# A preparation row of a fused attention, expert and slot kernel begins five turns later and is cut into seven pieces

## The chip, the cores and the metric

The kernel runs on one core of a Trainium2 chip. The metric is device time in microseconds (us) of one execution of the whole kernel. The profile is one execution taken by the hardware profiler; all positions in it are microseconds from the start of its span. The engines are named as the profile names them: PE (TensorE matmuls), PEld (TensorE weight loads), DVE (VectorE), ACT (ScalarE), POOL (GpSimd), SP (SyncE, which here only issues transfers).

## The reference, cut to what matters

`x` has 2048 tokens of 256 numbers, `ctx` has 1601 rows of 256. Four residual steps follow one another:

```python
x = x + cross_attention(layernorm(x), ctx)            # 16 heads, first stage
x = x + top1_of_8_experts(layernorm(x))               # second stage
x = x + windowed_attention(ctx, layernorm(x))         # third stage
x = x + slot_mixture(layernorm(x))                    # fourth stage
```

The third stage looks only at rows of `ctx` within 16 of a centre `p_t`, weighted by a Gaussian:

```python
mask = (idx < max(p_t - 16, 0)) | (idx > min(p_t + 16, src_len))
score = where(mask, -1e9, q @ W_a @ ctx.T)
align = softmax(score) * exp(-(idx - p_t)**2 / 128)
out = tanh(concat([align @ ctx, q]) @ W_c.T)
```

`p_t` and `src_len` are one number each, so everything that depends on them and on `ctx` alone (the window's rows, the mask, the Gaussian, the product of the rows with `W_a` and with `W_c`) is the same for all tokens. The kernel computes these tables once.

## The kernel before, in words

**Attention.** The first part of `body` runs to L909. Its last steps, after the last `weigh` (L907), are taken from a list `later` (L908): the last head group is transposed and divided (L798, L799), turned (L811 to L815), multiplied with `WoT` in two halves (L824), and each half is added to `x_sb` (L829). Both halves use the one PSUM buffer of `small()`, so the second half's matmuls wait until L829 has read the first half.

**The loads of the later stages.** SP issues 14 loads (L930 to L945). POOL issues the small ones (L947 to L965), among them `slen_i` (L947) and `pt` (L948, issued by the helper at L83).

**Experts, with rows beside them.** From L1400 the kernel walks five blocks of tokens: three of 4 x 128 tokens and two of 2 x 128 (`BLOCKS`, L967). `experts(lb)` (L1031) handles one 128-token tile at a time, in four pairs of experts. For one pair PE does two fp32 matmuls of 128x512 (four records in the profile, L1041) into one of four PSUM buffers, and DVE adds both experts to `x_sb` with two instructions (L1048). After each pair the generator yields. Behind every second tile an expert bias is added (L1059, L1061). A PSUM buffer comes free when L1048 or L1061 has read it.

Each yield of `experts` is one **turn**. In a turn, `aside(3)` (L1391) takes up to three rows (generators) from the front of the list `beside`, lets each do its next piece, and puts them at the end again. A row that ends does not count among the three. Nothing else sets the order: every engine executes its instructions in the order in which these pieces emit them. Only the end of attention and the beginning of this part are interleaved with one another when the program is built; the trace shows on each engine which came first. The rows are:

- `front(lb + 1)` (L1020): prepares the next block for the experts. Two pieces of layer-norm statistics (L990; DVE, then one POOL instruction L102 for the reciprocal root), two pieces that apply them (L995, which is L107 on DVE), two pieces that transpose on PE (L1002), two for the router (`route`, L147).
- `window()` (L1069): the tables of the third stage. This is the function that the change edits.
- `slots()` (L1246): tables of the fourth stage, in 7 pieces, added after block 0.
- `after(windowed(lb), weights(lb))`: the third stage and the fourth stage's weights of a block whose experts are done, added after each block. `windowed` reads the tables of `window` at L1194, in its seventh piece.

The rows that are left when the experts end are worked off one piece at a time (L1413), and the final slot computation and the output follow (L1416 to L1530).

**`window()` before.** Piece 1 (L1071 to L1094): `slen`, the window's limits `lo`, `hi` and `base` from `slen_i` and `pt` (seven DVE instructions, L1072 to L1083); the row numbers `at_i` (POOL iota L1086, DVE L1088 to L1090); and the gather of 64 rows of `ctx` with an indirect DMA issued by POOL (L1092). Piece 2 (L1112 to L1121): mask and Gaussian over the window's 64 rows. Piece 3 (L1124 to L1138): the same over all 1601 rows. Then empty turns. Then `eT` (L1142 to L1149: transposes of the gathered rows), `outside` (L1151 to L1158: 26 matmul records that sum all rows of `ctx`), `oT` and `m` (L1161 to L1178), and `evw` (L1180 to L1185). The pieces 1 to 3 run in turns 1 to 3, `eT` in turn 10, `evw` in turn 13.

Of the kernel before, what the change touches and what calls it, by code (L numbers as in the profile page):

```python
# [62 lines left out]
def body(ctx: ExitStack, tc: tile.TileContext, a: dict, out: bass.AP):  # L63
# [1004 lines left out]

    def window():  # L1069

        slen = late.tile([P, 1], F32, name="slen")  # L1071
        nc.vector.tensor_copy(slen, slen_i)  # L1072
        lo = late.tile([P, 1], F32, name="lo")
# [7 lines left out]
        base_i = late.tile([P, 1], I32, name="base_i")  # L1081
        nc.vector.tensor_copy(base_i, base)
        nc.vector.tensor_copy(base, base_i)  # L1083

        at_i = late.tile([NW, 1], I32, name="at_i")
        nc.gpsimd.iota(at_i, pattern=[[0, 1]], base=0, channel_multiplier=1)  # L1086
# [10 lines left out]
        def in_window(pos, n, name):  # L1097

            t = late.tile([P, n], F32, name=name)
            nc.vector.tensor_scalar(t, pos, lo, None, ALU.is_ge)  # L1100
            nc.vector.scalar_tensor_tensor(t, pos, hi, t, ALU.is_le, ALU.mult)
            return t

        def gauss(pos, n, name):
            t = late.tile([P, n], F32, name=name)
            nc.vector.tensor_scalar_sub(t, pos, pt)
            nc.vector.tensor_tensor(t, t, t, ALU.mult)
            nc.scalar.activation(t, t, AF.Exp, scale=-1.0 / 128.0)
            return t
# [4 lines left out]
        posr = late.tile([P, NW], F32, name="posr")  # L1114
        nc.vector.tensor_copy(posr, posr_i)
        nc.vector.tensor_scalar_add(posr, posr, base)
        inr = in_window(posr, NW, "inr")
        gr = gauss(posr, NW, "gr")
        neg = late.tile([P, 1, NK], F32, name="negw")
        nc.vector.tensor_scalar(neg[:, 0, :NW], inr, -1.0, 3e38, ALU.add, ALU.mult)  # L1120
# [9 lines left out]
        nc.gpsimd.iota(row_i, pattern=[[P, NS]], base=0, channel_multiplier=1)  # L1130
        row = late.tile([P, NS], F32, name="row")
        nc.vector.tensor_copy(row, row_i)
        ins = in_window(row, NS, "ins")
        gs = gauss(row, NS, "gs")
        nc.vector.tensor_scalar(ins, ins, -1.0, 1.0, ALU.mult, ALU.add)
# [1 line left out]
        one = late.tile([1, 1], F32, name="one")  # L1137
        nc.gpsimd.memset(one, 1.0)  # L1138

        for _ in range(7):  # L1140
            yield
        eT = late.tile([P, 2, NW], F32, name="eT")  # L1142
        gET = late.tile([P, 2, NK], F32, name="gET")
# [243 lines left out]

    NB = len(BLOCKS)
    beside = [window()]

    def aside(n):  # L1391
# [218 lines left out]
```

## Time and profile before

| what | value |
|---|---|
| time, median of 3 runs | 1083.15 us (1083.15 to 1085.77) |
| the profiled execution's own time | 1085.9 us |
| its span | 1084.1 us |
| PE busy in the span | 961.7 us (89%) |
| DVE busy in the span | 749.3 us (69%) |
| attention's last `acc` matmuls (L849) on PE | from 798.05 to 800.50 us |
| block 0's first pair of experts starts on PE | 800.40 us |
| block 0's last bias (L1059) starts on PE | 857.43 us |
| first addition of block 1 (L1048) | 860.44 us |
| first addition of block 2 (L1048) | 911.92 us |

A line of a timeline gives the start, the duration, the engine, the line of the kernel, the operation with its output and inputs, how many were merged, and in square brackets how long the engine had been idle and what ended that. In the chain of waits each line is a piece of the chain that ended last: start, length, engine and what it did. Tables by stretch give for each engine the busy time and the number of instructions, and then the clock that TensorE was granted (1.00 is full), the share of the DMA engines that was busy, and the GB/s.

### The profile page before, as it was taken

To read this page: it belongs to the slowest core of one execution; us is meant where nothing else is said; L and a number is where in the kernel's file an instruction comes from. 1 tells how busy PE (TensorE), PEld (TensorE's weight loads), DVE (VectorE), ACT (ScalarE), POOL (GpSimd) and SP (SyncE) were. 2 spreads that over 40 slices of the span, in tenths; PEclk is the share of its full clock that TensorE was granted. 3 is DMA by queue.
4 is the path that set the end of the run, shared out by engine and by line. 5 is a ranking of instruction groups with operands and counts; after the bars stand their busy time and mean duration, and the time that the engine had idled before them with its cause. 6 is when DMAs were issued, how large, how long until landed. Compare 5 with 4: busy or idle time off the path is not lost.

```text
span 1084.1 us, 14756 instructions
## 1 busy us (share of the span) xinstructions
PE 961.7 (89%) x5742; PEld 448.1 (41%) x5742; DVE 749.3 (69%) x1415; ACT 516.9 (48%) x614; POOL 71.9 (7%) x96
## 2 busy tenths in 40 slices
PE   6787888989989899898889989899997999999986
PEld 2234333444443343343334434344343455545543
DVE  6456867878777787878787876977016566675754
ACT  2423546666646565656566665665840011221331
POOL 4000200000010000001000000000020003021210
PEclk8777979999999999999999999998998999999999
DMA  4763721310102100001210110100033000000002
GB/s 157 162 150 93 145 71 44 107 27 3 28 2 71 60 13 28 16 13 28 88 29 2 28 28 2 28 2 1 2 108 116 1 1 0 1 1 1 1 0 78
DMA packets 32277, 46.96 MB, mean 43 GB/s; under 512 B 6412, under 2 KB 21269, under 8 KB 31951
## 3 DMA queue, kind: packets, MB, share of 16 engines
q1 hardware_dynamic: 30478, 43.65, 15.0%
q10 hardware_dynamic: 1232, 1.61, 0.4%
q8 instruction: 45, 0.74, 0.3%
q0 software_dynamic: 496, 0.76, 0.3%
q14 instruction: 26, 0.21, 0.1%
HBM read 26.77 MB, written 14.04 MB: 38 GB/s over the span
## 4 chain that ended last, share of the span: by engine, by line
PE 67%; DVE 24%; issue 4%; DMA 2%; ACT 1%; POOL 1%; SPq 0%; POOLq 0%; DVEq 0%; ACTq 0%
PE acc L849 18%; PE s_ps L883 14%; DVE mx L262 12%; PE a_ps L257 11%; PE y_ps L1041 7%; PE a_ps L240 2%; DVE xn L107 2%; DVE x_sb L1048 2%; PE a_ps L498 1%; PE a_ps L824 1%; PE o_ps L1227 1%; DVE ln_stats L96 1%; PE a_ps L284 1%; PE x_ps L461 1%; PE a_ps L461 1%
## 5 line engine op out<-in xcount | busy, mean ns | idle before, releaser
L262 DVE TENSOR_REDUCE mx<-a_ps 128x2 f32<-128x804 f32 (+1 forms) x645 | 494.2, 799 | 133.9 <-PE a_ps L257 123.4
L888 ACT ACTIVATE es<-s_ps 128x1024 f32<-128x1024 f32 (+1 forms) x416 | 405.6, 1021 | 231.8 <-PE s_ps L883 225.0
L257 PE MATMUL a_ps<-kb,qb 50*128 50x402 bf16 x992 | 235.3, 353 | 47.7 <-DVE mx L262 32.5
L883 PE MATMUL s_ps<-qt,kt 52*128 52x512 f32 (+1 forms) x832 | 242.4, 530 | 2.1 <-DMA qt<-nT 2.1
L849 PE MATMUL acc<-es,v 128*32 128x512 f32 (+1 forms) x1664 | 233.0, 632 | 0.0
L257 PEld LDWEIGHTS <-qb 50*128 50x128 bf16 x1024 | 81.2, 95 | 294.6 <-issue 276.3
L883 PE MATMUL s_ps<-ql,kt 52*128 52x512 f32 (+1 forms) x832 | 196.9, 403 | 0.0
L883 PEld LDWEIGHTS s_ps<-qt,kt 52*128 52x128 f32 (+1 forms) x832 | 102.9, 196 | 29.2 <-ACT es L888 16.1
L883 PEld LDWEIGHTS s_ps<-ql,kt 52*128 52x128 f32 (+1 forms) x832 | 108.5, 192 | 0.4
L1041 PE MATMUL y_ps<-expert_wT_sb,xT 128*128 128x512 f32 x192 | 89.8, 598 | 0.0
L102 POOL TENSOR_TENSOR ln_rstd<-ln_ve,mhalf 128x2 f32<-128x2 f32 (+2 forms) x28 | 21.1, 754 | 781.3 <-DVE ln_ve L100 780.0
L1048 DVE SCALAR_TENSOR_TENSOR x_sb<-y_ps,r_gate,x_sb 128x256 f32<-128x256 f32 x96 | 46.3, 482 | 32.5 <-PE y_ps L1041 30.7
L849 PEld LDWEIGHTS acc<-es,v 128*32 128x32 f32 (+1 forms) x1664 | 33.4, 109 | 54.5 <-issue 52.9
L1041 PEld LDWEIGHTS y_ps<-expert_wT_sb,xT 128*128 128x128 f32 x192 | 34.1, 191 | 31.9 <-issue 30.8
L1004 ACT COPY xT<-tr_ps 128x512 f32<-128x512 f32 (+1 forms) x28 | 13.4, 493 | 53.3 <-PE tr_ps L1001 53.3
L798 DVE RECIPROCAL rec<-a_ps 128x16 f32<-128x16 f32 x16 | 4.1, 258 | 49.4 <-PE a_ps L240 49.4
L107 DVE TENSOR_SCALAR xn<-x_sb,ln_mv,ln_rstd 128x256 f32<-128x256 f32 x64 | 32.8, 554 | 1.1 <-POOL ln_rstd L102 1.1
L1041 PE MATMUL y_ps<-expert_wT_sb,xnT 128*128 128x512 f32 x64 | 32.2, 631 | 0.0
L1001 PE MATMUL tr_ps<-ident,xn 128*128 128x128 f32 x88 | 17.6, 296 | 10.9 <-DVE xn L107 10.9
L284 PE MATMUL a_ps<-ident,nsp 128*8 128x128 f32 x64 | 10.0, 279 | 19.3 <-DVE nsp L275 18.9
L96 DVE BATCH_NORM_STATS2 ln_stats<-x_sb 128x6 f32<-128x256 f32 x64 | 23.3, 413 | 3.4 <-POOL x_sb L1235 3.4
L1048 DVE SCALAR_TENSOR_TENSOR x_sb<-y_ps,gate,x_sb 128x256 f32<-128x256 f32 x32 | 15.4, 483 | 13.6 <-PE y_ps L1041 13.0
(343 smaller groups left out, 727.9 us busy)
## 6 DMA issues: line engine op xcount, KB each, us to landing
qt<-q_rows SPq DMA_DIRECT2D x32, 192.0 KB
q_rows<-qhi SPq DMA_DIRECT2D x8, 512.0 KB
qb<-q_rows SPq DMA_DIRECT2D x30, 96.0 KB
kt<-expert_wT_sb SPq DMA_DIRECT2D x24, 100.5 KB
q_rows<-qp SPq DMA_DIRECT2D x8, 256.0 KB
q_rows<-qlo SPq DMA_DIRECT2D x8, 256.0 KB
ql<-q_rows SPq DMA_DIRECT2D x32, 64.0 KB
expert_wT_sb<-in_expert_wT SPq DMA_DIRECT2D x1, 2048.0 KB
```

The lines of the kernel that those rows point to most:

```text
L96: nc.vector.bn_stats(stats[:rows, i, :], src[:, i, :])
L102: nc.gpsimd.tensor_tensor(rstd[:rows, :n], ve[:rows, :n], mhalf[:rows, :n], ALU.pow)
L107: nc.vector.tensor_scalar(dst[:, i, :], src[:, i, :], mv[:rows, i, 0:1], rstd[:rows, i : i + 1], ALU.subtract, ALU.mult,)
L240: nc.tensor.transpose(ps[:, t * P : (t + 1) * P], src[:, t, c * P : c * P + n], ident)
L257: nc.tensor.matmul(ps[:, k, :CH], qb[u % 2][rows, pl, t * P : (t + 1) * P], kb[g][rows, pl, c * CH : (c + 1) * CH], start=True, stop=True,)
L262: nc.vector.tensor_reduce(flat[:, n : self.n], ps[:, : self.n - n, :CH], AX.X, ALU.max)
L461: nc.tensor.matmul(ps[:n, :D], ctxT[:, c, i * P : i * P + n], wv[:, c, :], start=c == 0, stop=c == 1,)
L849: nc.tensor.matmul(acc[HP * j : HP * (j + 1), :], v[:n, i, h * VW : h * VW + HP], es[j // 2][:n, j % 2, :], start=i == 0, stop=i == NS - 1,)
L883: nc.tensor.matmul(ps[:n, h, :], kt[u % NG][rows, pl, i * P : i * P + n], q[u % nq][rows, pl, :], start=k == 0, stop=k == 1,)
L888: nc.scalar.activation(e[:n], ps[:n], AF.Exp)
L1041: nc.tensor.matmul(ps.rearrange("p e d -> p (e d)"), xT[:, c, tok], ew[:, c, pair * 2 * D : (pair + 1) * 2 * D], start=c == 0, stop=c == 1,)
L1048: nc.vector.scalar_tensor_tensor(xb[:, t, :], ps[:, k, :], gate[:, t, e : e + 1], xb[:, t, :], ALU.mult, ALU.add,)
```

## The change

`window()` first yields five times with nothing done. Its three pieces of tables become seven: the limits alone; the row numbers and the gather; the positions; the mask; the Gaussian; the sums and the positions of all rows; their mask and Gaussian. The run of yields ahead of `eT` is cut from seven to four. No instruction is added, removed or given another size.

```diff
     def window():
 
+
+        for _ in range(5):
+            yield
         slen = late.tile([P, 1], F32, name="slen")
...
         nc.vector.tensor_copy(base, base_i)
+        yield
 
         at_i = late.tile([NW, 1], I32, name="at_i")
...
         nc.vector.tensor_scalar_add(posr, posr, base)
+        yield
         inr = in_window(posr, NW, "inr")
+        yield
         gr = gauss(posr, NW, "gr")
...
         nc.vector.tensor_copy(row, row_i)
+        yield
         ins = in_window(row, NS, "ins")
...
-        for _ in range(7):
+        for _ in range(4):
             yield
         eT = late.tile([P, 2, NW], F32, name="eT")
```

## The prediction

> **What bounds the kernel now.** I read the busy shares first (PE 89%, DVE 69%), then the chain of waits, then the stretch where the edited row stands. PE is the longest engine almost everywhere, so time can only be won where PE stands still. The slices of the page show PE falling to 7 tenths beside the start of the expert stage, near 810 us. The chain of waits from 800 to 832 us:
>
> ```profile
> 800.52 0.59 ACT osb L787
> 801.13 0.78 POOL slen_i L947
> 801.91 6.94 DMA pt_b<-in_pt
> ...
> 809.78 0.61 DVE x_sb L829
> 810.43 2.01 PE a_ps L824 x8
> ...
> 823.33 0.80 PE tr_ps L1001 x2
> 824.13 3.41 PE y_ps L1041 x4
> 827.54 0.83 PE tr_ps L1001 x4
> 828.37 1.72 PE y_ps L1041 x4
> 830.09 1.69 PE r_ps L155 x16
> ```
>
> The chain leaves PE for a tiny transfer (`pt`, 6.94 us) and returns to it for good only at 823.33. Also, four matmuls of a pair take 3.41 us at 824.13 and 1.72 us at 828.37. The timeline of PE names the idle time:
>
> ```profile
> 810.43 1.99 PE L824 MATMUL a_ps<-WoT_sb,aT 128*128 128x256 f32 x8 [1.45 <-DVE x_sb L829]
> 820.02 0.65 PE L1001 MATMUL tr_ps<-ident,xn 128*128 128x128 f32 x2 [3.72 <-DVE xn L107]
> 823.33 0.80 PE L1001 MATMUL tr_ps<-ident,xn 128*128 128x128 f32 x2 [2.66 <-DVE xn L107]
> ```
>
> All three waits are for DVE. The timeline of DVE says why it is late:
>
> ```profile
> 808.02 0.15 DVE L1072 CAST slen<-slen_i 128x1 f32<-128x1 int32 x1 [2.89 <-DMA slen_i<-in_slen]
> 808.88 0.15 DVE L1074 TENSOR_SCALAR lo<-pt_b 128x1 f32<-128x1 f32 x1 [0.70 <-DMA pt_b<-in_pt]
> ...
> 814.01 0.99 DVE L1048 SCALAR_TENSOR_TENSOR x_sb<-y_ps,gate,x_sb 128x256 f32<-128x256 f32 x2
> ```
>
> Piece 1 of `window` stands in DVE's queue ahead of both L829 and of the second pair's additions (814.01, though PE had that pair done near 805). DVE waits for two transfers with everything behind it. Last, the table by stretch (clock is third from the end):
>
> ```profile
> 816.30:820.00 3.70, 0.00 (x0) 0.00 (x0) 2.74 (x11) 0.26 (x1) 0.95 (x6) 1.00 1.01 344
> 820.00:823.30 3.30, 0.65 (x2) 0.28 (x2) 2.92 (x14) 0.68 (x2) 0.00 (x0) 0.71 0.95 285
> 823.30:828.30 5.00, 4.97 (x11) 2.66 (x12) 1.86 (x5) 0.58 (x1) 0.00 (x0) 0.51 0.02 5
> ```
>
> PE's two pauses are followed by 5 us at half clock. From 830.09 to 857.43 (the block's last bias) the chain is PE without a pause, 27.34 us; block 1 (860.4 to 911.9) has only 1.6 us of PE idle.
>
> **The opening of block 0 after the change.** Turns 1 to 5 carry nothing of `window`. I lay out DVE and PE with the trace's durations: pair 1.72 us on PE, its two additions 1.0, statistics of two tiles 1.25 (0.74 + 0.30 + 0.2), applying them 0.73, L829 0.69.
>
> - PE runs as before to the end of the first L824 half, near 808.0. DVE has meanwhile done pair 1 and the second statistics (805.2 to 807.5), so L829 runs at 808.05 instead of 809.70 and the second L824 half starts near 808.9 instead of 810.43: 1.5 us won. Should L829 stand behind one more addition, 1.0 of this is lost.
> - PE goes on: second half to 810.8, pair 3 to 812.5, gate transposes to 813.0, pair 4 to 814.75.
> - The first transposes need the first applied tiles, and these need POOL's reciprocal root. This is the next thing that is late:
>
> ```profile
> 812.63 0.13 POOL L1240 MEMSET xn<- 128x16 f32 x1 [0.34 <-PE a_ps L824]
> 812.70 0.73 POOL L102 TENSOR_TENSOR ln_rstd<-ln_ve,mhalf 128x2 f32<-128x2 f32 x1
> ```
>
> This is the first of two roots; before, the second waited for DVE until 816.16. The first can hardly start earlier, because POOL issues loads until 812.30 and that doesn't change. With the second directly behind it, the roots end at about 813.1 and 813.85. DVE: apply 813.2 to 813.9, pair 3's additions to 814.9, second apply to 815.6. PE: first two transposes at 814.75, the others at 815.65, done at 816.0 with 0.55 us of idle time.
> - Then pair 5, transposes, pair 6: 1.72 + 0.6 + 1.72, so `r_ps` starts near 820.0 against 830.09. PE's own work from 800.4 to there checks it: 7 pairs 12.0, L240 1.8, L824 3.9, gate 0.5, transposes 1.2, in all 19.4, so 819.8 without any idle time.
>
> The winnings are 1.5 (L824) + 3.72 + 2.66 - 0.55 = 5.8 (pauses) + 2.4 (the clock), 9.7 us.
>
> For the clock, the row says PE worked 4.97 us at 0.51, so 2.4 us is lost. The Trainium skill ("TensorE: Matmul & The Clock Gate", Part 1: The HAM clock gate) says half clock comes after an idle window of some 3.4 us and goes after some 3.4 us of sustained work; by that 1.7 us would be lost, and the sum would be 9.0. I take the row.
>
> A rule speaks against this. The skill ("SBUF — State Buffer", two separate sides) says DVE and POOL share a port pair as an exclusive lock, and POOL cannot write descriptors while certain DVE instructions run. DVE is now to work from 805 to 812 while POOL issues loads, where it used to wait. By the rule, each of POOL's five issues from 808.28 to 811.75 could wait for one DVE instruction, up to 0.5 us each: root 2.5 us later, transposes at 816.5 or so, gain 7.5. But the rows show POOL's issues at 0.53 to 0.56 us from 802.46 to 805.11, where DVE ran additions and statistics, and 0.52 to 0.55 where it stood. I take zero, and keep 2.5 for the range.
>
> **Where the removed work lands.** The seven pieces come in turns 6 to 12. Their DVE time by start-to-start distances: limits 1.0, row numbers 0.5, window tables 1.56, all-row tables 1.75, in all 4.8 us. Cover: PE in turns 6 to 12 has 7 pairs 12.0, transposes 0.6, router 1.7, bias 1.1 = 15.4. DVE there has additions 6.7, router 1.95, bias 0.7 and the 4.8, 14.1. It fits, with four PSUM buffers of slack; adding turn by turn, DVE is at most some 3 us behind PE (turn 12). Cost zero; without cover 4.8. The transfers `slen` and `pt` landed by 808.9, the limits now run near 819: no wait.
>
> The gather moves from POOL at 814.37 to near 823, behind the loads and roots instead of between the two roots (one reason why the second was late). Its issue takes 1.01 us and it lands in 6.7; `eT` reads it nine turns later, at least 15 us. SP's 14 loads keep their place and are all issued by 818.7; nothing of `window` stands in SP's queue. Cost zero. If the gather took over 15 us, PE would wait for the rest.
>
> `eT` moves from turn 10 to turn 16, and `outside`, `oT`/`m`, `evw` (PE 5.71 + 0.53 + 1.03 + 0.86 = 8.13 us) from turns 11 to 13 to turns 17 to 20, block 1. PE is the bound in both blocks, so this only moves. There is one new wait: DVE's copy of `outside` stood idle 4.70 us for PE in block 0, which had room. In block 1, `slots` and statistics of the third stage queue behind it. DVE in turns 17 to 22: six pairs' additions 5.7 (0.95 each), four statistics 5.0, four applies 2.9, `slots` 2.8 (L1250 to L1278), `window` 1.3, bias 0.7, wait 4.7 = 23.1. PE: six pairs 10.3, `window` 8.1, `slots` 5.2, bias, gate and transposes 3.4 = 27.0. It fits: zero, if not, up to 4.7.
>
> In turns 17 to 20 four rows share three visits per turn, so `front`, `slots` and the third stage each fall one turn back. Counting visits, block 0's row ends in turn 42 instead of 41 and from turn 43 the order is the old one. The tail is the same instruction for instruction: zero. Block 1's 1.6 us of PE idle may partly fill: up to 1.6 more.
>
> **Rivals.** (1) *DVE becomes the bound in turns 6 to 12*: all 4.8 us reach the path; gain 4.9, 1078.3. Against it: 14.1 under 15.4. (2) *The interleaving puts an L829 behind the first apply, which waits for POOL's root*: L829 at 813.9, second L824 half at 814.6, PE idle 5.7 us and perhaps half clock again; gain 2 to 5, about 1079.5. Against it: in the trace both L829 come before instructions that waited for POOL. (3) *Slower*: DVE waits for `outside` in block 1 with the densest DVE stretch behind it. Price 4.7, with 4.8 uncovered in block 0 and one pair's time (1.72) for rows that fall back: 11.2 against 9.7, +1.5, 1084.7. It decides once PE's waits for DVE in turns 6 to 24 pass 9.7 us. Against it: 23.1 under 27.0. (4) *Nothing changes*, because the first root is the real bound: then PE would still reach `r_ps` near 830. Against it: that root ended at 813.43 and PE was free from 816.3, yet the transposes came at 820.02.
>
> **How the numbers follow.** The profiled execution took 1085.9 (span 1084.1, 1.8 around it): less 9.7 is 1076.2. It lies 2.75 above the median, to which I apply the same difference: 1083.15 - 9.7 = 1073.4. Chances: full gain (7.5 to 12) 0.72; rival 1 or 2, gain 3.3 to 7.5, 0.19; about no change 0.04; slower 0.05. A difference under 0.3% (3.2 us) can't be told from none. The range goes from 1070.5 (idle of block 1 filled too, 1.6, and a little DVE smoothing) to 1079.0 (rival 1 and most of 2).
>
> **What would show it.** Right: no DVE wait for `slen` or `pt`; L829 near 808; `tr_ps` starting near 815 with idle below 1 us; no stretch at 0.5 clock from 815 to 830; `r_ps` near 820; `out_ps` behind block 1's first pair; the first addition of block 2 near 902. Wrong: PE waiting for L1048 in turns 7 to 13 (rival 1), L829 at 813 or later (rival 2), PE idle after `out_ps` (rival 3), `r_ps` near 830 (rival 4).

## The result, and the profile after

Median time after 1077.57 us (1077.25 to 1077.90, four runs) against 1083.79 before (four runs): ratio 0.9938, interval 0.9911 to 0.9965. Forecast was 1073.4 with a range of 1070.5 to 1079.0. The profiled execution after took 1077.58 us, its span is 1075.8.

The chain of waits after the change, from the end of attention (start, length, what):

```profile
802.92 1.06 PE y_ps L1041 x2
...
808.76 1.81 PE a_ps L824 x8
...
811.43 1.92 PE a_ps L824 x8
...
817.22 0.44 PE tr_ps L1001 x4
817.66 1.72 PE y_ps L1041 x4
819.38 0.44 PE tr_ps L1001 x4
819.81 1.72 PE y_ps L1041 x4
821.53 1.69 PE r_ps L155 x16
```

PE never leaves the chain. From the first pair of experts to the router it takes 18.5 us (802.85 to 821.37 in PE's timeline); before it took 29.5 (800.40 to 829.92). The table by stretch for the same three windows as before (clock third from the end):

```profile
816.30:820.00 3.70, 3.70 (x16) 2.01 (x15) 2.43 (x7) 0.74 (x2) 0.00 (x0) 1.00 1.11 296
820.00:823.30 3.30, 3.30 (x21) 2.50 (x20) 2.21 (x10) 0.43 (x1) 0.00 (x0) 1.00 1.05 366
823.30:828.30 5.00, 5.00 (x14) 2.17 (x14) 3.91 (x19) 0.23 (x1) 1.36 (x5) 1.00 0.49 152
```

No pause and full clock. DVE's timeline shows where the waits went (line numbers after the edit are 3 to 7 higher below L1068; the limits are L1075 on):

```profile
810.61 0.69 DVE L829 TENSOR_TENSOR x_sb<-x_sb,a_ps 128x512 f32<-128x512 f32 x1 [1.06 <-PE a_ps L824]
...
814.92 0.73 DVE L107 TENSOR_SCALAR xn<-x_sb,ln_mv,ln_rstd 128x256 f32<-128x256 f32 x2 [0.85 <-POOL ln_rstd L102]
...
820.33 0.14 DVE L1075 CAST slen<-slen_i 128x1 f32<-128x1 int32 x1
...
849.00 0.41 DVE L1165 COPY outside<-out_ps 1x256 f32<-1x256 f32 x1 [3.62 <-PE out_ps L1161]
```

L829 waits for PE alone, the limits wait for nothing, and the copy of `outside` now waits in block 1. POOL's first root, the next thing expected to be late, comes 11.3 us after the first pair of experts (12.3 before), and the second follows it at once:

```profile
814.06 0.15 POOL L1247 MEMSET xn<- 128x16 f32 x1
814.13 1.55 POOL L102 TENSOR_TENSOR ln_rstd<-ln_ve,mhalf 128x2 f32<-128x2 f32 x2
```

**Two measures of the same change.** The first pair of experts starts at 802.85 after and at 800.40 before, though up to there both are the same program. Counted from that pair, the rest takes 283.70 us before (1084.1 - 800.4) and 272.95 after: 10.75 won. The two profiled times differ by 8.3, because 2.45 went ahead of the edited code. Most experiments below are therefore read from the first pair on, and their medians stand beside it.

### The profile page after: what moved, and what is told of

It is laid out like the page before. It is cut to its first block, busy times and chain, and to the rows that moved or that the text cites. A ratio compares the mean times of both kernels' runs of the same rounds, so it can differ in the third digit from the quotient of the medians.

```text
span 1075.8 us, 14758 instructions
## 1 busy us (share of the span) xinstructions
PE 960.7 (89%) x5742; PEld 448.5 (42%) x5742; DVE 750.1 (70%) x1415; ACT 517.2 (48%) x614; POOL 72.0 (7%) x96
## 3 DMA queue, kind: packets, MB, share of 16 engines
q10 hardware_dynamic: 1232, 1.61, 0.4%
## 4 chain that ended last, share of the span: by engine, by line
PE 70%; DVE 22%; issue 4%; DMA 1%; ACT 1%; SPq 1%; POOL 0%; POOLq 0%; DVEq 0%; ACTq 0%
PE acc L849 18%; PE s_ps L883 14%; DVE mx L262 12%; PE a_ps L257 11%; PE y_ps L1041 8%; PE a_ps L240 2%; PE a_ps L824 2%; PE a_ps L498 1%; DVE xn L107 1%; PE o_ps L1234 1%; DVE x_sb L1048 1%; DVE ln_stats L96 1%; PE a_ps L284 1%; PE x_ps L461 1%; PE a_ps L461 1%
## 5 line engine op out<-in xcount | busy, mean ns | idle before, releaser
L849 PE MATMUL acc<-es,v 128*32 128x512 f32 (+1 forms) x1664 | 232.7, 631 | 0.0
L1048 DVE SCALAR_TENSOR_TENSOR x_sb<-y_ps,r_gate,x_sb 128x256 f32<-128x256 f32 x96 | 46.3, 482 | 37.9 <-PE y_ps L1041 36.0
L849 PEld LDWEIGHTS acc<-es,v 128*32 128x32 f32 (+1 forms) x1664 | 33.4, 109 | 54.3 <-issue 52.8
L107 DVE TENSOR_SCALAR xn<-x_sb,ln_mv,ln_rstd 128x256 f32<-128x256 f32 x64 | 33.2, 562 | 1.9 <-POOL ln_rstd L102 1.9
L1041 PE MATMUL y_ps<-expert_wT_sb,xnT 128*128 128x512 f32 x64 | 29.6, 597 | 0.0
L96 DVE BATCH_NORM_STATS2 ln_stats<-x_sb 128x6 f32<-128x256 f32 x64 | 23.4, 413 | 3.4 <-POOL x_sb L1242 3.4
L262 DVE TENSOR_REDUCE mx<-s_ps 128x2 f32<-128x804 f32 x16 | 15.9, 994 | 12.5 <-PE s_ps L257 12.5
L974 PE MATMUL busy_ps<-xnT 128*128 128x512 bf16 x95 | 24.2, 387 | 0.0
```

The costliest lines, as they stand in the source:

```text
L96: nc.vector.bn_stats(stats[:rows, i, :], src[:, i, :])
L107: nc.vector.tensor_scalar(dst[:, i, :], src[:, i, :], mv[:rows, i, 0:1], rstd[:rows, i : i + 1], ALU.subtract, ALU.mult,)
L262: nc.vector.tensor_reduce(flat[:, n : self.n], ps[:, : self.n - n, :CH], AX.X, ALU.max)
L849: nc.tensor.matmul(acc[HP * j : HP * (j + 1), :], v[:n, i, h * VW : h * VW + HP], es[j // 2][:n, j % 2, :], start=i == 0, stop=i == NS - 1,)
L974: nc.tensor.matmul(calm[0].rearrange("p e d -> p (e d)"), xnT[:, 1, :P].bitcast(BF16)[:, 1::2], xnT[:, 0, :].bitcast(BF16)[:, 1::2], start ...
L1041: nc.tensor.matmul(ps.rearrange("p e d -> p (e d)"), xT[:, c, tok], ew[:, c, pair * 2 * D : (pair + 1) * 2 * D], start=c == 0, stop=c == 1,)
```

## The experiments

All durations in this table are from each kernel's profile, in us from the first `y_ps` matmul on PE: to the router's first matmul (`r_ps`), and to the end of the span. "First pair" is where that matmul lies in the span. Where an expectation counts from the start of attention's last weighing matmul (L849), that is 0.5 us earlier; where it counts from attention's end, it is the same within 0.1 us.

| kernel | first pair | to router | to end | median | ratio to before (95%) |
|---|---|---|---|---|---|
| before | 800.40 | 29.52 | 283.70 | 1083.79 | |
| b_again | 799.01 | 29.33 | 283.39 | 1085.82 | 0.9997 (0.9985 to 1.0009) |
| warm | 798.98 | 27.34 | 283.22 | 1085.04 | 0.9993 (0.9974 to 1.0012) |
| early_loads | 800.39 | 27.09 | 281.11 | 1084.42 | 0.9977 (0.9964 to 0.9991) |
| pieces_only | 800.38 | 25.24 | 280.32 | 1084.09 | 0.9968 (0.9951 to 0.9985) |
| delay1 | 800.42 | 23.31 | 277.48 | 1080.00 | 0.9946 (0.9930 to 0.9963) |
| delay2 | 801.76 | 20.63 | 277.04 | 1077.86 | 0.9931 (0.9911 to 0.9952) |
| after | 802.85 | 18.52 | 272.95 | 1077.57 | 0.9938 (0.9911 to 0.9965) |
| a_again | 798.99 | 18.72 | 273.11 | 1077.09 | 0.9909 (0.9891 to 0.9927) |
| a_third | 797.93 | 18.52 | 272.87 | 1072.53, one run | |
| delay_only | 799.03 | 18.73 | 272.67 | 1074.56 | 0.9884 (0.9856 to 0.9912) |
| in_block0 | 799.80 | 18.70 | 273.10 | 1073.67 | 0.9886 (0.9869 to 0.9904) |
| in_block0_again | 798.70 | 18.52 | 273.00 | 1073.50, one run | |
| delay8 | 802.74 | 18.84 | 272.26 | 1076.57 | 0.9904 (0.9877 to 0.9932) |

**Both kernels again.** No edit. On record for the kernel before:

> The kernel before, unchanged, for a second profile. In the first pair of profiles the part up to attention's first weighing matmul (L849) is the same program, yet it started at 102.2 us before and at 104.6 after. Theory A (the early loss belongs to an execution: the TensorE clock rises earlier or later): this profile may show either 102 or 105, and its time goes with it, 1083 to 1086. Theory B (the early loss belongs to the changed program): 102.2 again. Both: the two pauses of PE behind the attention (3.7 and 2.7 us) and the half clock behind them are there again.

And for the changed one:

> The changed kernel, unchanged, for a second profile. Theory A: L849 first starts at 102 or at 105, as it falls. Theory B: 104.6 again. Time 1077 to 1078; no PE pause over 0.5 us between the attention's end and the second block, full clock there.

Theory A holds in its main point: the early loss belongs to an execution. The first weighing matmul started at 104.7 us in b_again and at 100.4 in a_again, the reverse of the first pair of profiles; the first pair of experts lay between 797.93 and 802.85 over all profiles, early and late with either program. From that pair on, each of the two kernels repeats within about 0.3 us. One clause of theory A failed: the time does not go with L849's start, for b_again began L849 2.4 us later than before and was still at its first pair of experts 1.4 us earlier. The time of the changed kernel also reached below what I expected of it (1073.86). The scatter arises in two places. One is ahead of L849. The same window of the first stage in before, after and a_again, one view each:

```profile
20.00:50.00 30.00, 25.34 (x67) 8.02 (x65) 12.14 (x13) 11.25 (x17) 0.00 (x0) 0.67 0.61 136
```

```profile
20.00:50.00 30.00, 25.34 (x65) 7.83 (x64) 11.62 (x13) 11.26 (x17) 0.00 (x0) 0.61 0.56 127
```

```profile
20.00:50.00 30.00, 23.98 (x68) 7.56 (x66) 13.64 (x15) 12.33 (x19) 0.00 (x0) 0.72 0.71 164
```

The granted clock is 0.67, 0.61 and 0.72, and L849 first starts at 102.2, 104.6 and 100.4. The other place lies between L849 and the first pair of experts, a stretch of 698.1 us in before and 694.4 in b_again. The same window in these two:

```profile
105.00:200.00 95.00, 83.27 (x548) 35.10 (x547) 73.67 (x115) 52.36 (x57) 6.81 (x10) 0.91 0.36 83
```

```profile
105.00:200.00 95.00, 82.38 (x562) 34.37 (x554) 75.14 (x118) 52.68 (x58) 6.82 (x10) 0.96 0.39 91
```

Over all fourteen profiles, let the clock lost be the sum of (1 - granted share) x time over the trace's clock records. From L849 to the first pair, the three profiles that lost 19.5 us of clock took 694.3 to 694.4 us, the two that lost 23.3 to 23.4 took 695.6 to 695.9, and the nine that lost 26.8 to 28.5 took 698.1 to 698.6. So the order agrees with the clock in both places. That the clock is the cause was not tried.

**The late start alone**: three pieces, not seven.

```diff
+        for _ in range(5):
+            yield
         slen = late.tile([P, 1], F32, name="slen")
...
-        for _ in range(7):
+        for _ in range(8):
             yield
```

> Only the late start: three pieces as before, in turns 6 to 8, eT in turn 16 as in the changed kernel. My theory (the whole gain is that DVE waits for no load or POOL result in turns 1 to 5): the router's first matmul 18.6 us after the attention's last one ends, as in the changed kernel, time 1077 to 1078.5. Rival (the cutting carries part of the gain, since DVE would fall behind PE with three longer pieces): PE waits for L1048 in turns 7 to 10, time 1079 to 1082.

18.7 us to the router and 272.7 to the end: all of the gain, with whole pieces. The median, 1074.56, is lower than the 1077 to 1078.5 that I gave, and the ratio's interval overlaps that of a_again. The cutting contributes nothing that shows.

**The cutting alone**: the changed kernel without its empty turns, `eT` in turn 10 as before.

```diff
-        for _ in range(5):
-            yield
         slen = late.tile([P, 1], F32, name="slen")
...
-        for _ in range(4):
+        for _ in range(3):
             yield
```

> Only the cutting: seven pieces from turn 1 on, eT in turn 10 as before. The limits still wait for slen and pt ahead of L829, but the second pair's additions and second statistics stand ahead of the row numbers that wait for POOL. My theory: L829 stays late (1.5 us lost), the rest of the pause shrinks to 1 to 3 us without the half clock; time 1079 to 1082, router's first matmul 20.5 to 23.5 us after the attention's end. Rival (the cutting is what gains): 1077 to 1078. Rival (only the start counts): as before, 1083.5.

25.2 us to the router: a part of the gain, less than my 20.5 to 23.5, and the time is above the 1079 to 1082 that I gave. The term I missed is the interleaving: the second pair's additions and statistics now stand behind the waiting limits and ahead of L829. The half clock was not gone either: from 814 to 817 us the granted clock was 0.51, and the second L824 half took 2.94 us instead of 1.99. PE's and POOL's timelines:

```profile
812.60 2.94 PE L824 MATMUL a_ps<-WoT_sb,aT 128*128 128x256 f32 x8 [3.64 <-DVE x_sb L829]
```

```profile
815.75 0.13 POOL L1244 MEMSET xn<- 128x16 f32 x1 [4.09 <-PE a_ps L824]
```

PE's pause moves to L824, and POOL waits for L824 before the memset that stands ahead of both roots. A wait of DVE thus comes back to DVE through PE and POOL.

**The load's wait alone**: `slen_i` and `pt` come during attention.

```diff
                         load_experts()
+                        nc.sync.dma_start(slen_i, a["slen"].partition_broadcast(P))
+                        nc.sync.dma_start(pt, a["pt"].partition_broadcast(P))
...
-    nc.gpsimd.dma_start(slen_i, a["slen"].partition_broadcast(P))
-    pt = load_rows(late, "pt")
```

> The row of window as before, but slen and pt are loaded by SP during attention (with the experts' weights) instead of by POOL behind it, so the limits wait for no load. Measured from the start of attention's last weighing matmul to the router's first matmul (30.0 us before, 19.1 after). My theory (the load is only the first of several waits; the row numbers then wait for POOL, and the window's DVE work stands ahead of the second pair's additions): 27 to 29 us, time 1 to 3 us below before. Rival (the load's wait is the whole cause): 19 to 21 us, as in the changed kernel.

POOL issues two loads fewer in it, too. 27.1 us to the router, 2.4 less than before (27.6 by the count on record, inside 27 to 29). DVE's timeline:

```profile
804.91 0.15 DVE L1073 CAST slen<-slen_i 128x1 f32<-128x1 int32 x1
...
808.15 0.69 DVE L831 TENSOR_TENSOR x_sb<-x_sb,a_ps 128x512 f32<-128x512 f32 x1 [2.19 <-PE a_ps L826]
...
812.03 0.15 DVE L1089 CAST at<-at_i 64x1 f32<-64x1 int32 x1 [0.42 <-POOL at_i L1087]
...
812.47 0.98 DVE L1049 SCALAR_TENSOR_TENSOR x_sb<-y_ps,gate,x_sb 128x256 f32<-128x256 f32 x2
```

The limits wait for nothing and the first half is added on time, yet the second pair's additions come at 812.47, because the row numbers ahead of them wait for POOL's iota. The load is the first wait of the chain of waits, and less than a quarter of the loss, even with POOL's two loads fewer counted to it.

**One and two empty turns**, three pieces (`range(1)` in delay1):

```diff
+        for _ in range(2):
+            yield
         slen = late.tile([P, 1], F32, name="slen")
```

> Three pieces as before, starting one turn later (turns 2 to 4), all else moved with them. My theory (what counts is how many turns pass before DVE meets POOL's queue): stretch from the last weighing matmul to the router 23 to 26 us. Rival (any delay past the load's landing is enough): 19 to 20.5 us. Rival (only the whole five turns help): 28 to 30 us.

> Three pieces as before, starting two turns later (turns 3 to 5). My theory: the first application of the statistics stands ahead of the limits now, and the row numbers find POOL nearly free: 20 to 22 us for the same stretch. Rival (only five turns help): 24 us or more.

23.3 and 20.6 us to the router (23.8 and 21.1 by the count on record): both as I expected, and outside what the rivals gave. The gain grows turn by turn. In delay1 DVE still waits for the two loads (0.59 and 1.09 us), so this kernel does not yet test a start behind their landing; delay2 does. DVE also still meets POOL's queue in delay1:

```profile
814.32 0.14 DVE L1090 CAST at<-at_i 64x1 f32<-64x1 int32 x1 [1.08 <-POOL at_i L1088]
```

In delay2 no instruction of the three pieces waits any more for a load or for POOL's row numbers. They only stand ahead of the second applying and of the additions, and PE still waits for L107:

```profile
818.03 0.65 PE L1001 MATMUL tr_ps<-ident,xn 128*128 128x128 f32 x2 [1.68 <-DVE xn L107]
```

**The clock alone**: matmuls of no use fill the pauses of the kernel before (13 ahead of the first of these transposes, 9 ahead of the third), and so add work without changing what is waited for.

```diff
             for t in range(nt):
+                for _ in range({0: 13, 2: 9}.get(t, 0) if warm is not None else 0):
+                    nc.tensor.matmul(
+                        warm, xnT[:, 1, :P].bitcast(BF16)[:, 1::2],
+                        xnT[:, 0, :].bitcast(BF16)[:, 1::2], start=True, stop=True,
+                    )
                 nc.tensor.transpose(
```

> The kernel before with 22 matmuls of no use (128x512, bf16, into a PSUM buffer nobody reads) where PE stands still: 13 ahead of the first transposes of block 1's tokens, 9 ahead of the third. They fill the two pauses and don't end them. It separates the clock from the pauses. My theory (5 us at half clock cost 2.4 us): granted clock 1.00 from 816 to 832, the stretch from the last weighing matmul to the router 27.2 to 28 us instead of 30.0. Rival (the half clock costs nothing that shows, since PE is not the bound there): 29.5 to 30.5 us.

27.34 us to the router, 2.2 less than before and 2.0 less than b_again, with the pauses as long as they were. So the half clock behind the pauses cost 2.0 to 2.2 us. But to the end only 0.5 of it is left (0.2 against b_again). The tables by stretch of warm, in block 0 and in block 1:

```profile
816.00:820.00 4.00, 3.20 (x15) 1.26 (x13) 3.75 (x16) 0.26 (x1) 0.00 (x0) 1.00 1.08 343
820.00:824.00 4.00, 3.37 (x12) 1.41 (x11) 2.83 (x9) 1.26 (x3) 0.00 (x0) 1.00 0.32 103
824.00:828.00 4.00, 4.00 (x25) 2.88 (x24) 1.94 (x4) 0.59 (x1) 0.00 (x0) 1.00 0.01 2
...
880.00:884.00 4.00, 4.00 (x16) 2.34 (x14) 1.37 (x4) 0.65 (x2) 0.00 (x0) 0.61 0.00 0
884.00:888.00 4.00, 3.67 (x10) 1.34 (x8) 2.95 (x13) 0.00 (x0) 0.00 (x0) 0.96 0.00 0
```

A spell at half clock (a stretch with a granted clock of 0.5) comes in block 1, where before had none: (1 - 0.61) x 2 x 4 + (1 - 0.96) x 2 x 4 = 3.4 us long, so 1.7 us lost. From first addition to first addition, block 1 took 53.18 us instead of 51.49.

**Where the window's PE work stands.** Late start in three pieces, with `evw` done in turn 14 of block 0:

```diff
+        for _ in range(5):
+            yield
         slen = late.tile([P, 1], F32, name="slen")
...
-        for _ in range(7):
+        for _ in range(3):
             yield
```

> The late start (three pieces in turns 6 to 8), but eT in turn 11 and evw in turn 14, so that all of the window's PE work stays in block 0 and no other row falls back a turn in block 1. Measured from the first pair of experts on PE. Theory (moving that work into block 1 only moves it): the router at 18.5 us and the end of the span within 1 us of the changed kernel's (272.9 us after the first pair; 272.8 in delay_only), apart from half-clock spells that differ by execution. Rival (the move into block 1 carries part of the gain by filling idle time there): 1 to 2 us longer. Rival (the move costs): 1 to 2 us shorter.

And the changed kernel, still later:

```diff
-        for _ in range(5):
+        for _ in range(8):
             yield
```

> The changed kernel with eight empty turns instead of five: eT in turn 19, evw in turn 22, one turn before the third stage reads the tables. Theory: the gain is over once the first turns are free, so the router stays at 18.5 us from the first pair; in block 1 the rows fall back further, by 0 to 2 us in all. Rival (the slower case of the prediction: DVE waits for the sum of all rows in block 1's densest stretch): PE waits for DVE there, 3 us or more longer.

18.7 and 18.8 us to the router, 273.1 and 272.3 to the end. The slower case doesn't come: even with `out_ps` in turn 20, nothing of the size of 3 us is lost. in_block0 has no spell at half clock in the expert stage in either profile, while after, a_again, a_third and delay_only each have one; equal ends with and without a spell mean that the move does win something. The distances between the blocks' first additions (L1048) show it. In in_block0_again block 0 and block 1 take 46.50 + 51.49 = 97.99 us and block 2 takes 50.55, as before (50.55). In after it is 37.91 + 59.22 = 97.13 without a spell there, and 51.02 in block 2 with one; in a_again it is 38.12 + 60.84 = 98.96 with the spell, and 49.33 in block 2 without. So a spell costs 60.84 - 59.22 = 1.6 or 51.02 - 49.33 = 1.7, and the move into block 1, with the rows falling back one turn, wins 0.9 in the first two blocks and 1.2 in block 2. PE's idle time (the stretch less PE's busy time) shows where: in block 2 it is 3.26 us in before and in in_block0_again, but 2.15 in after and a_again. In block 1 it did not shrink (1.61 against 2.02 and 1.95).

**Is it the spell?** Both once more, for their profiles:

> The changed kernel once more, for its profile. In both profiles so far one spell of 3.4 us at half clock fell into block 1 or 2, at different places (872 to 880, 920 to 928), and from the first pair of experts to the end took 272.9 and 273.1 us. Theory (a spell costs 1.7 us and comes as it falls; without it the move of the window's PE work into block 1 shows): 271.2 to 271.5 us without a spell, 272.9 to 273.1 with one, 274.6 with two. Rival (spells cost nothing there): 273.0 in any case.

> The late start with the window's PE work kept in block 0, once more. Its first profile had no spell at half clock and 273.1 us from the first pair to the end. Theory: 273.1 without a spell, 274.8 with one. Rival (spells cost nothing): 273.1 in any case.

272.87 with one spell, 273.00 without: what the theory says, but the rival says the same, since the changed kernel had a spell again. These two runs decide nothing; the block distances above do. What the clock did in a_third, PE's timeline and then the table by stretch:

```profile
868.07 1.85 PE L155 MATMUL r_ps<-router_wT_sb,xT 128*128 128x8 f32 x16
869.77 1.98 PE L1205 MATMUL s_ps<-m,xT 128*128 128x65 f32 x16
871.68 1.13 PE L1059 MATMUL eb_ps<-eb,gT 8*128 8x256 f32 x4
872.74 5.40 PE L1041 MATMUL y_ps<-expert_wT_sb,xT 128*128 128x512 f32 x8
```

```profile
868.00:872.00 4.00, 4.00 (x35) 3.83 (x33) 1.75 (x6) 0.23 (x1) 0.00 (x0) 1.00 0.01 4
872.00:876.00 4.00, 4.00 (x8) 1.68 (x7) 1.67 (x4) 0.42 (x1) 0.00 (x0) 0.63 0.00 0
```

PE is busy throughout, with narrow matmuls, and the clock drops all the same. The same instructions stand in the same order in block 1 of the first profile of the changed kernel, and there they kept the full clock (after, PE's timeline):

```profile
872.99 1.85 PE L155 MATMUL r_ps<-router_wT_sb,xT 128*128 128x8 f32 x16
874.70 1.98 PE L1205 MATMUL s_ps<-m,xT 128*128 128x65 f32 x16
876.60 1.13 PE L1059 MATMUL eb_ps<-eb,gT 8*128 8x256 f32 x4
877.66 3.70 PE L1041 MATMUL y_ps<-expert_wT_sb,xT 128*128 128x512 f32 x8
```

The two pairs take 3.70 us there and 5.40 in a_third: 1.7 us again. So the sequence alone doesn't bring the spell.

## Why the prediction came out as it did

It was right in sign and mechanism, and the time lies in its range. The number is in part luck: a gain of 6.2 us falls among those that the prediction kept for rivals 1 and 2 (3.3 to 7.5), and neither of them came. Step by step:

- *L829 earlier, 1.5 us.* The second L824 half starts 10.03 us after the first pair of experts before (810.43) and 8.50 after (811.35): 1.53. Right.
- *Pauses, 5.8 us.* All 6.4 us (3.72 + 2.66) are gone, the remaining 0.55 didn't come: the root was 1.0 us earlier than I placed it against the first pair. My floor for PE (19.4 us to the router) was also too high, since it took 18.5: I summed durations of records that overlap.
- *Clock, 2.4 us by the row, 1.7 by the rule.* warm measures 2.0 to 2.2 for this place, between the two. By the prediction's own rows the half clock lasted (1 - 0.71) x 2 x 3.3 + (1 - 0.51) x 2 x 5 = 6.8 us, of which PE worked some 5; the estimate of 1.7 had put 3.4 us of work into it. These three terms sum to 9.9 to 10.1 of the 11.0 us won up to the router; the rest is not assigned. What I didn't see is that the clock can fall again: with the pauses gone, a spell of 3.4 us comes in block 1 or 2 in all three profiles of the changed kernel and takes 1.7 back. Its length is what the Trainium skill gives for one window of the gate ("TensorE: Matmul & The Clock Gate", Part 1: The HAM clock gate), but no PE pause preceded the spell of a_third.
- *Port lock, 0 to 2.5 us.* Zero was right: POOL's issues took 0.52 to 0.75 us with DVE working beside them, as before.
- *Window's DVE work in turns 6 to 12 at no cost.* PE's timeline has one line for the pairs of these turns, without a wait:

```profile
826.02 14.00 PE L1041 MATMUL y_ps<-expert_wT_sb,xnT 128*128 128x512 f32 x32
```

- *PE work into block 1 only moves, up to 1.6 more from idle time of block 1.* It won 2.1 us over blocks 0 to 2 (0.9 + 1.2), but not from that idle time, which grew from 1.6 to 2.0 us; in block 2, PE's idle time fell from 3.26 to 2.15. The spell took 1.7 of the gain.
- *The copy of `outside`*: waited 3.62 us, hidden, as I summed.
- *The tail, zero.* From block 4's first addition to the end it took 92.8 us in all three profiles of the changed kernel, against 92.1 and 92.2 in the two of the kernel before. Up to the output's matmuls (`f_ps`) PE starts the same work within 0.01 us in before and after; the 0.6 us lie behind them, with the output's additions and stores. Why stays open.

Of the rivals, DVE as the bound, the late L829, the slower case and the first root as the bound did not come; the late L829 behind other work did come in pieces_only, by the mechanism of rival 2 with additions in place of the root.

The sum from the first pair on was 9.7 and is 10.3 to 10.8. The median difference is 6.2 all the same, so 1077.57 and not 1073.4. The term that was mis-sized is not in the edited code: it is the median of three runs, 1083.15, from which the prediction subtracts. I applied the difference to a median of runs whose first 800 us differ by up to 4.9 us from execution to execution. By the profiles, 1.8 us around the span and 272.9 from the first pair on, the four runs after (1077.25 to 1077.90) would have started that pair at 802.5 to 803.2, the latest seen; the run before at 1083.15 at some 797.8, the earliest. Of these runs only the one at 1077.58 has a profile (802.85), so for the others this is worked out and not shown. What is on record fits it: in the later comparison 40 runs of the kernel before had a median of 1085.91 (1080.03 to 1090.68), 2.8 us above the 1083.15, and the ratio was 0.9909, which is 9.9 us with 1.9 either way (the two medians are 8.8 apart), and fits 10.7.

Open stays what sets the granted clock ahead of the edited code, with which attention's early or late end goes, and what decides where a spell falls. No variant is clearly better than the changed kernel: delay_only and in_block0 have the lower medians, but their intervals overlap with a_again's and their times from the first pair on are the same within 0.5 us.

## What to carry to other kernels

In a strict queue, side work that waits for a late load or another engine's queue should not stand ahead of work whose result the bound engine needs. Count how many instructions stand behind the wait, and through which engines it comes back; the load that heads the chain may be the least of it (2.4 of 10.8 us here). When a sum is tested against a median, measure from the last point that both programs share, since executions here differ by 4.9 us before they reach the edit.

## What the runs showed of the hardware that I had not expected

TensorE's granted clock fell to half for some 3.4 us in the expert stage with no long pause of PE to explain it: in a_third behind 3.7 us of narrow matmuls (128x8 and 128x65) without any pause, in after among the narrow matmuls that follow a pause of 1.90 us:

```profile
921.47 2.06 PE L1205 MATMUL s_ps<-m,xT 128*128 128x65 f32 x14 [1.90 <-ACT xT L1004]
```

Neither is enough by itself: the sequence of a_third kept the full clock in after, and that of after kept it in a_again (919.44, the same pause of 1.90). Such a spell came in the expert stage in all three profiles of the changed kernel and in delay_only, delay2 and warm, but not in in_block0 (twice), delay1 or delay8.

POOL's ninth load in a row waited for its first to land in every profile: `bsq` for `slen_i`, 2.2 to 3.0 us, in thirteen of them. In early_loads, where POOL issues two loads fewer, `bsq` did not wait, and the ninth there, `bsv`, waited 2.52 us for the first, `b1`. The roots follow behind these loads on POOL.
